# Two groups of attention heads share their transposes, and the largest scores run ten steps ahead instead of six

## The chip, the cores and the metric

The kernel runs on one core of a Trainium2 chip. A core has engines that each work through their own queue in order and wait for one another by semaphores: TensorE (PE in the profile, its weight loads PEld), VectorE (DVE), ScalarE (ACT), GpSimd (POOL), and SyncE (SP), which issues most of the DMA transfers. PE writes to PSUM, a small memory of eight banks; DVE and ACT read PSUM, POOL doesn't here. The metric is the device time of one execution in microseconds (us); the runs of a kernel are given by their median.

## The reference

Two transformer blocks with adaptive layer norm over x of 8 batches x 512 tokens x 128 channels, all in fp32. Only the first block's attention is touched:

```python
h = _layernorm(x) * (1 + ca) + sa
Q = lora(h, Wq...).reshape(N, S, 16, 8)          # 16 heads of 8 channels; K and V alike
energy = einsum("nqhd,nkhd->nhqk", Q, K) / sqrt(8)
attn = softmax(energy, axis=-1)
out = einsum("nhqk,nkhd->nqhd", attn, V).reshape(N, S, 128)
x = x + ga * lora(out, Wo...)
```

After it come a mixture of experts (8 experts, the best 2 for each token, and a shared one), a state-space layer and a second mixture of experts with a small feed-forward part. The softmax is computed as exp(score - largest score of the query) divided by the sum of these.

## The kernel before

**Groups, steps and slots.** A batch `b` has 16 heads. Four of them make a group: in group `g = 4b + m` the heads are 4j + m for j = 0 to 3, and head j uses the partitions 32j to 32j + 31 of PE, so the four heads of a group are four row groups of the array. There are 32 groups. A group has four steps, one for each 128 keys (`t = 4g + kc`), and a step has two slots (`s = 2t` and `2t + 1`), one for each half of the heads. `slot(s)` (L893) writes one slot: `scores` (two matmuls 32x512 of keys by queries, tile `ps`), `maxima` for a later step (two matmuls of queries by keys, tile `pm`, in the two row groups that the scores leave free), the two exponentials on ACT (`exps`, tile `es`), the reduction of `pm` on DVE to the largest score, and then everything that was put behind this slot.

**The order of the rest** is written out by hand: `at_slot(s, do)` (L606) appends a piece of work to slot s, and within a slot pieces stand in the order in which they were appended. All engines get their instructions in this order (`keep_in_program_order`), and each waits for its own operands only.

**Largest scores.** `LEAD = 6` (L286): in step t the maxima of step t + 6 are computed. Before step 0 the first six steps' maxima are done alone by `maxima_first` (L495), four matmuls and three reductions each. `split(g)` (L465) makes the group's queries `qt` and keys `kt` by masking `qf` and `kf`, 8 rows of each 32 in use; one spare row of `kt` (at `r0`) is set to 1. The reductions write into the columns of `mpad`, a tile that is zero elsewhere. `max_done(g)` (L514), in slot 8g - 3, transposes the group's `mpad` with four matmuls (`pmt`) and subtracts the result from `qt` on DVE, so that the spare row of `qt` holds minus the largest score, which the score matmul then adds. There are four `mpad` tiles and three buffers each for `qt` and `kt`.

**Weighted sums.** `values(b)` (L451) puts the values of a batch into `vaug`, 32 columns for each head: 8 values, a 1 in column 8 (it gives the sum of the exponentials), and zeros. `weigh(g, qc)` (L544) multiplies the exponentials by it, 16 matmuls for each 128 queries (tile `av`), and ACT copies the result (32 rows for each head, 9 of them in use) into `part`. This is done in slots 9, 11, 12 and 13 from the group's first. `normalise(g)` (L564), in slot 8g + 15, transposes `part` with four matmuls (`ppt`); DVE takes the reciprocal of the sums and multiplies.

**Around it**, for each batch: `load_stats`, `load_root`, `load_batch` (layer norm: DVE statistics, POOL square root and scaling `xh`, PE transposes `ptn`, ACT modulation `ht`), `project_batch` (`pqk`, then ACT makes `qf` and `kf`), `values` (`pv`), `channels_back` and `out_proj` (`pot`, `py`), `out_stats`, and then the routing for the experts: `tokens` (POOL and ACT), `turn` (`ptf`), `route` (`pl`), `choose`, `place` (`pcount`), and eight `scatter`s, indirect DMA transfers that POOL issues every second slot. `table` (L797) makes the list of expert blocks in slots 237 to 255.

**PSUM.** The pool `sc` has four buffers of a bank (`bank`), which `ps`, `av`, `pmt`, `ppt` and most other matmuls take in turn; `mx` has two buffers of two banks (`pair`) for `pm` and `pqk`.

Two lines set the number of steps ahead and where the two transposes stand:

```python
            at_slot(8 * g - 3, lambda g=g: max_done(g))          # L611
            at_slot(8 * g + 15, lambda g=g: normalise(g))        # L614
```

Of the kernel before, what the change touches and what calls it, by code (L numbers as in the profile page):

```python
# [10 lines left out]
FP = mybir.dt.float32  # L11
# [3 lines left out]
ALU = mybir.AluOpType  # L15
# [4 lines left out]
P = 128  # L20
# [48 lines left out]
def tile_adaln_two_blocks(  # L69
# [211 lines left out]

    mv1, rs1 = new_stats("l0a")
    mv2, rs2 = new_stats("l0f")
    LEAD = 6  # L286
    STEPS = 4 * 4 * B
    ES = 28
    kp = ctx.enter_context(tc.tile_pool(name="kp", bufs=1, side="right"))
# [2 lines left out]
    with tc.tile_pool(name="at", bufs=2) as at, tc.tile_pool(name="sc", bufs=4, space=PSUM) as psc, tc.tile_pool(  # L292
# [5 lines left out]
        for i in range(2):  # L298
            va = ate.tile([P, NC4, 16, 32], FP, tag=f"vaug{i}", name=f"vaug{i}")
            G.memset(va, 0.0)  # L300
            G.memset(va[:, :, :, HD], 1.0)
            vaugs.append(va)

        def pair(name):
# [5 lines left out]
        def flat(ps):  # L310
            return ps.rearrange("p c t -> p (c t)")
# [139 lines left out]
        def values(b):  # L451
            ht = batch[b]["ht"]
            ps = bank("pv")
            for c in range(NC4):
                pin(
                    T.matmul(
                        ps[:, c, :], lhsT=ht[:, c * P : (c + 1) * P], rhs=wqk[:, 2, :], start=True, stop=True
                    )
                )
            A.copy(  # L460
                vaugs[b % 2].rearrange("p c h r -> p (c h) r")[:, :, 0:HD],
                flat(ps).rearrange("p (c d) -> p c d", d=HD),
            )

        def split(g):  # L465

            b, m = g // 4, g % 4
            sp = (m + 1) % 4
            qt = ate.tile([P, S], FP, tag="qt", name="qt", bufs=3)
            kt = ate.tile([P, S], FP, tag="kt", name="kt", bufs=3)  # L470
            (V if g == 0 else G).tensor_scalar(qt, batch[b]["q"], mask[:, m : m + 1], zero, ALU.mult, ALU.add)
            G.tensor_scalar(kt, batch[b]["k"], mask[:, m : m + 1], spare[:, sp : sp + 1], ALU.mult, ALU.add)
            group[g] = (qt, kt)

        def maxima(u, half):

            g, qc = u // 4, u % 4
            qt, kt = group[g]
            r0 = HD * ((g + 1) % 4)
            pm = pair("pm")  # L480
            for i in range(2):
                r = 32 * (2 * half + i)
                pin(
                    T.matmul(  # L484
                        pm[:, i, :],
                        lhsT=qt[r : r + 32, qc * P : (qc + 1) * P],
                        rhs=kt[r : r + 32, :],
                        start=True,
                        stop=True,
                    )  # L490
                )
            mp = mpads[g % 4][:, qc, :].rearrange("p (j r) -> p j r", r=32)
            return lambda: V.tensor_reduce(mp[:, 2 * half : 2 * half + 2, r0], pm, AX.X, ALU.max)

        def maxima_first(u):  # L495

            g, qc = u // 4, u % 4
            qt, kt = group[g]
            r0 = HD * ((g + 1) % 4)
            pm = pair("pm")  # L500
            banks = [pm[:, 0, :], pm[:, 1, :], flat(bank("pm")), flat(bank("pm"))]
            for j, ps in enumerate(banks):
                r = 32 * j
                pin(
                    T.matmul(
                        ps, lhsT=qt[r : r + 32, qc * P : (qc + 1) * P], rhs=kt[r : r + 32, :], start=True, stop=True
                    )
                )
            mp = mpads[g % 4][:, qc, :].rearrange("p (j r) -> p j r", r=32)
            V.tensor_reduce(mp[:, 0:2, r0], pm, AX.X, ALU.max)  # L510
            for j in (2, 3):
                V.tensor_reduce(mp[:, j : j + 1, r0], banks[j], AX.X, ALU.max)

        def max_done(g):  # L514

            qt, _ = group[g]
            pt = bank("pmt")
            for c in range(NC4):
                pin(T.transpose(pt[:, c, :], mpads[g % 4][:, c, :], ident))  # L519
            V.scalar_tensor_tensor(qt, flat(pt), -1.0, qt, ALU.mult, ALU.add)  # L520

        def scores(t, half):
            g, kc = t // 4, t % 4
# [20 lines left out]
        def weigh(g, qc):  # L544

            b, m = g // 4, g % 4
            q = slice(P * qc, P * qc + P)
            ps = bank("av")
            for kc in range(NC4):
                for j in range(4):  # L550
                    pin(
                        T.matmul(  # L552
                            ps[32 * j : 32 * j + 32, 0, :],
                            lhsT=vaugs[b % 2][:, kc, 4 * j + m, :],
                            rhs=es_of[4 * g + kc, j][:, q],
                            start=(kc == 0),
                            stop=(kc == NC4 - 1),
                        )
                    )
            if qc == 0:  # L560
                part_of[g] = at.tile([P, NC4, P], FP, tag="part", name="part")
            A.copy(part_of[g][:, qc, :], ps[:, 0, :])

        def normalise(g):  # L564

            b, m = g // 4, g % 4
            part = part_of.pop(g)
            pt = bank("ppt")
            for c in range(NC4):
                pin(T.transpose(pt[:, c, :], part[:, c, :], ident))  # L570
            if m == 0:
                batch[b]["o"] = at.tile([P, NC4, D], FP, tag="o", name="o", bufs=1)
            p4 = pt.rearrange("p c (j r) -> p c j r", r=32)
            rd = stat.tile([P, NC4, 4], FP, tag="rd", name="rd")
            V.reciprocal(rd, p4[:, :, :, HD])
            o4 = batch[b]["o"].rearrange("p c (j m d) -> p c j m d", j=4, m=4)[:, :, :, m, :]
            V.tensor_tensor(o4, p4[:, :, :, 0:HD], rd.unsqueeze(3).to_broadcast([P, NC4, 4, HD]), ALU.mult)

        def channels_back(b):
            o = batch[b]["o"]  # L580
# [25 lines left out]
        def at_slot(s, do):  # L606
            after.setdefault(s, []).append(do)

        for g in range(4 * B):
            at_slot(8 * g - 16, lambda g=g: split(g))  # L610
            at_slot(8 * g - 3, lambda g=g: max_done(g))  # L611
            for qc in range(NC4):
                at_slot(8 * g + (9, 11, 12, 13)[qc], lambda g=g, qc=qc: weigh(g, qc))
            at_slot(8 * g + 15, lambda g=g: normalise(g))  # L614

        at_slot(-42, silu_c)
        for t, n in ((-41, 9), (-31, 5), (-22, 3), (-16, 8), *((t, 5) for t in range(-11, 0, 2))):
            at_slot(t, lambda n=n: keep_busy(n))
        at_slot(-34, low_rank)
        at_slot(-33, lambda: modulation(0, mod0))  # L620
        at_slot(1, lambda: clamp(mod0, MOE_SCALE))
        at_slot(2, out_bias)
        at_slot(-9, lambda: modulation(1, mod1))
        at_slot(6, lambda: clamp(mod1, None))
        rows = ((gab, gab_rows), (mod0[:, 2, :], ga_rows), (mod0[:, 3, :], sb_rows), (mod0[:, 4, :], cb_rows))
        for i, (src, dst) in enumerate(rows):
# [1 line left out]
            at_slot(8 + i, lambda dst=dst, i=i: mod_rows_in(dst, i))  # L628
        for b in range(B):
            for c in range(NC4):  # L630
                at_slot(32 * b - 40 + c, lambda b=b, c=c: load_stats(b, c))
            if b == 0:
                at_slot(-35, lambda: load_root(0, 0))
                at_slot(-32, lambda: load_root(0, 1))
            else:
                at_slot(32 * b - 35, lambda b=b: load_root(b))
            for i, s in enumerate((-30, 20, -24)):
                at_slot(32 * b + s, lambda b=b, i=i: load_batch(b, i))
            for i in range(2):
# [1147 lines left out]
```

## Time and profile before

| | |
|---|---|
| three runs, median (lowest to highest) | 1055.69 us (1055.5 to 1057.73) |
| the profiled execution | 1081.55 us |
| its span, mean clock granted to PE | 1079.6 us, 0.97 |
| busy in the span: PE, DVE, ACT, POOL | 1004.6, 668.8, 637.0, 486.7 us |
| first maxima at, first scores at | 18.51, 37.40 us |
| one batch of 32 slots in the steady part | 63.8 us |
| experts' first block begins | 548.7 us |

A row of a group reads: line, engine, operation, output <- inputs, shape and count, then busy time and mean ns of one, then idle time of the engine ahead of it and what ended it. L65 is the helper through which DVE, ACT, POOL and SP instructions are recorded, so these are told apart by their tiles. In windows, a row is start and end, length, busy time of PE, PEld, DVE, ACT and POOL with counts, then granted clock, DMA share and GB/s. In the chain of waits and the timeline, a row begins with start and duration in us. An fp32 matmul appears as two records, a transpose as one.

### The profile page before, as it was taken

Reading aid. Unit: us, or ns where it says so; the run is one execution under the profiler, and the core shown is the slowest. Engines: PE = TensorE matmul, PEld = TensorE weight load, DVE = VectorE, ACT = ScalarE, POOL = GpSimd, SP = SyncE. Lnnn points to the kernel's source line nnn. Section 1 sums busy time; section 2 is a strip of 40 time slices with the busy share of each in tenths; the row PEclk is TensorE's granted clock in tenths of the full one; section 3 lists DMA queues with packets and bytes.
Section 4 is the critical chain, followed back from the end, with each engine's and each line's share of the span. In section 5 each row is a group of like instructions: output and inputs, shape, how many; then the busy total and the mean of one; then the engine's idle time right before and its main releaser. Section 6 shows DMA issues by size and latency. Waiting matters only on the chain.

```text
span 1079.6 us, 24180 instructions
## 1 busy us (share of the span) xinstructions
PE 1004.6 (93%) x9522; PEld 658.2 (61%) x9522; DVE 668.8 (62%) x1297; ACT 637.0 (59%) x1400; POOL 486.7 (45%) x764
## 2 busy tenths in 40 slices
PE   9999999999999999999989999869899967767988
PEld 7555555555555555555579899748778634344556
DVE  6967787777768777777321123035766359888663
ACT  1466676666767666676745656225586563675554
POOL 3313142554627445454453133546441374666662
PEclk9999999999999999999999999969999968999999
DMA  6099200000000000000237796412553043213051
GB/s 168 20 315 283 88 12 2 11 22 2 31 1 20 13 9 24 2 30 10 71 114 221 230 275 196 127 35 64 146 152 89 8 131 99 79 59 126 23 186 39
DMA packets 94769, 95.36 MB, mean 88 GB/s; under 512 B 7664, under 2 KB 72560, under 8 KB 94656
## 3 DMA queue, kind: packets, MB, share of 16 engines
q1 hardware_dynamic: 90384, 85.13, 26.4%
q0 software_dynamic: 4096, 8.40, 2.6%
q8 instruction: 75, 1.23, 0.5%
q10 hardware_dynamic: 176, 0.30, 0.1%
q14 instruction: 38, 0.31, 0.1%
HBM read 62.43 MB, written 31.36 MB: 87 GB/s over the span
## 4 chain that ended last, share of the span: by engine, by line
PE 75%; DVE 10%; POOL 5%; ACT 4%; issue 4%; DMA 1%; SPq 0%; DVEq 0%; ACTq 0%; POOLq 0%
PE ps L531 21%; PE av L552 11%; PE pyb L1044 9%; PE ph L1033 8%; PE pm L484 3%; PE pmt L519 2%; PE r L1441 2%; PE pw L1352 2%; PE ppt L570 2%; DVE t L65 1%; DVE xc L65 1%; PE idle L417 1%; PE pe L1453 1%; PE pqk L444 1%; PE pyb L1003 1%
## 5 line engine op out<-in xcount | busy, mean ns | idle before, releaser
L65 DVE TENSOR_REDUCE mpad<-pm 128x2 f32<-128x1024 f32 (+1 forms) x262 | 310.3, 1194 | 110.2 <-PE pm L484 107.1
L65 ACT ACTIVATE es<-ps 128x512 f32<-128x512 f32 x512 | 275.6, 598 | 158.7 <-PE pm L484 135.0
L531 PE MATMUL ps<-qt,kt 32*128 32x512 f32 x1024 | 291.2, 630 | 0.7 <-DVE x L65 0.6
L484 PE MATMUL pm<-kt,qt 32*128 32x512 f32 x976 | 261.5, 636 | 0.0
L552 PEld LDWEIGHTS av<-es,vaug 128*32 128x32 f32 x4096 | 104.2, 109 | 94.1 <-ACT part L65 42.5
L552 PE MATMUL av<-es,vaug 128*32 128x128 f32 x4096 | 137.7, 276 | 0.0
L531 PEld LDWEIGHTS ps<-qt,kt 32*128 32x128 f32 x1024 | 94.0, 183 | 61.4 <-issue 30.6
L65 ACT ACTIVATE hid<-ph,bias 128x256 f32<-128x256 f32 x184 | 72.3, 478 | 58.0 <-PE ph L1033 56.2
L786 POOL DMA_INDIRECT x_rows<-tok,ux x64 | 65.0, 1015 | 68.4 <-DMA x_rows<-tok,ux 61.8
L1044 PEld LDWEIGHTS pyb<-w2b,hid 128*128 128x128 f32 x736 | 91.1, 194 | 5.8 <-ACT hid L65 2.4
L1044 PE MATMUL pyb<-w2b,hid 128*128 128x128 f32 x736 | 91.9, 278 | 2.6 <-ACT hid L65 2.0
L1033 PE MATMUL ph<-xt,w1b 128*128 128x256 f32 x368 | 89.9, 388 | 1.7 <-issue 1.7
L1064 POOL DMA_INDIRECT yg<-y_rows,yrows x64 | 63.3, 989 | 38.1 <-DMA hl<-h_chan 19.0
L484 PEld LDWEIGHTS pm<-kt,qt 32*128 32x128 f32 x976 | 73.1, 183 | 8.7 <-ACT kf L65 5.4
L1453 PE MATMUL pe<-x,l1w_sb 128*128 128x512 f32 x128 | 70.4, 663 | 5.3 <-ACT ye L65 5.3
L1033 PEld LDWEIGHTS ph<-xt,w1b 128*128 128x128 f32 x368 | 68.3, 195 | 9.8 <-issue 2.1
L65 DVE COPY xt<-pxt 128x256 f32<-128x256 f32 x46 | 19.2, 419 | 88.8 <-PE pxt L958 77.2
L65 POOL TENSOR_SCALAR qt<-qf,mask,zero 128x512 f32<-128x512 f32 x31 | 23.9, 772 | 109.4 <-PE pm L484 92.9
L65 ACT ACTIVATE ye<-pe,pc 128x512 f32<-128x512 f32 x64 | 43.2, 684 | 36.9 <-PE pe L1453 34.6
L65 POOL TENSOR_TENSOR t<-t 128x512 f32<-128x512 f32 x34 | 48.0, 1413 | 23.3 <-DVE t L65 21.8
L65 DVE TENSOR_TENSOR t<-ye,gb 128x512 f32<-128x512 f32 x64 | 55.0, 882 | 2.6 <-POOL t L65 2.3
L1441 PE MATMUL r<-l1w_sb,t 128*128 128x128 f32 x240 | 34.3, 290 | 15.2 <-POOL t L65 11.9
(298 smaller groups left out, 1559.4 us busy)
## 6 DMA issues: line engine op xcount, KB each, us to landing
x_rows<-zeros SPq DMA_DIRECT2D x16, 1024.0 KB
gb<-g_rows SPq DMA_DIRECT2D x32, 512.0 KB
w1b<-in_w1t SPq DMA_DIRECT2D x46, 256.0 KB
w2b<-in_w2t SPq DMA_DIRECT2D x46, 256.0 KB
xg<-x_rows SPq DMA_DIRECT2D x46, 128.0 KB
y_rows<-yb SPq DMA_DIRECT2D x46, 128.0 KB
x<-in_x SPq DMA_DIRECT2D x8, 256.0 KB
h_chan<-hf SPq DMA_DIRECT2D x8, 256.0 KB
```

Source lines behind the costliest of these rows:

```text
L65: return lambda *args, **kwargs: self.pin(call(*args, **kwargs))
L484: T.matmul(pm[:, i, :], lhsT=qt[r : r + 32, qc * P : (qc + 1) * P], rhs=kt[r : r + 32, :], start=True, stop=True,)
L519: pin(T.transpose(pt[:, c, :], mpads[g % 4][:, c, :], ident))
L531: T.matmul(ps, lhsT=kt[r : r + 32, kc * P : (kc + 1) * P], rhs=qt[r : r + 32, :], start=True, stop=True)
L552: T.matmul(ps[32 * j : 32 * j + 32, 0, :], lhsT=vaugs[b % 2][:, kc, 4 * j + m, :], rhs=es_of[4 * g + kc, j][:, q], start=(kc == 0), stop=( ...
L570: pin(T.transpose(pt[:, c, :], part[:, c, :], ident))
L786: nc.gpsimd.indirect_dma_start(out=x_rows[h], out_offset=IndirectOffsetOnAxis(ap=chosen["ux", b][:, k, c : c + 1], axis=0), in_=half[h]["t ...
L1033: pin(T.matmul(ph[:, f, :], lhsT=it["w1"][:, f * P : (f + 1) * P], rhs=it["x"], start=True, stop=True))
L1044: T.matmul(py[:, c, :], lhsT=it["hid"][:, f, c * P : (c + 1) * P], rhs=it["w2"][:, f, :], start=(f == 0 and "shared" not in it), stop=(f = ...
L1064: nc.gpsimd.indirect_dma_start(out=gathered[b][:, k, c, :], out_offset=None, in_=y_rows[h], in_offset=IndirectOffsetOnAxis(ap=half[h]["yro ...
L1441: T.matmul(ffn[b]["r"][:, c, :], lhsT=x[:, c * P : (c + 1) * P], rhs=w, start=(start and c == 0), stop=stop, skip_group_check=True,)
L1453: pin(T.matmul(pe, lhsT=l1w_sb[:, 2 + e, :], rhs=x1s[b], start=True, stop=True))
```

## The change

Groups are taken in pairs, 2n and 2n + 1.

- The spare row of a group is moved by 16, (m + 2) mod 4 in place of (m + 1) mod 4, and both groups of a pair write their largest scores into one `mpad` (two tiles in place of four). `max_done` is called for even groups only, in slot 8g - 3: four transposes, then two subtractions, one for each group's `qt`.
- In `vaug` the heads of odd m have their values in columns 16 to 23 and the 1 in column 24. ACT copies the weighted sums of an even group into `part` as before; those of the odd group are added to the same `part` by DVE. `normalise` is called for even groups only, in slot 8g + 23, and handles both.
- For that the maxima of two groups must be known before the first begins: `LEAD` is 10, ten steps of `maxima_first` stand ahead of step 0 (with five idle matmuls behind each), `qt` and `kt` have four buffers, and `split` and all that it needs are put eight slots earlier (`values` six, `modulation(1)` four).

```diff
-    for m in range(4):
+    for m in range(2):
         mp = ct([P, NC4, P], f"mpad{m}")
...
-    LEAD = 6
+    LEAD = 10
...
-            G.memset(va[:, :, :, HD], 1.0)
+            for e in range(2):
+                G.memset(va.rearrange("p c (n e) r -> p c n e r", e=2)[:, :, :, e, 16 * e + HD], 1.0)
...
-            A.copy(
-                vaugs[b % 2].rearrange("p c h r -> p (c h) r")[:, :, 0:HD],
-                flat(ps).rearrange("p (c d) -> p c d", d=HD),
-            )
+            for e in range(2):
+                A.copy(
+                    vaugs[b % 2].rearrange("p c (n e) r -> p (c n) e r", e=2)[:, :, e, 16 * e : 16 * e + HD],
+                    flat(ps).rearrange("p (n e d) -> p n e d", e=2, d=HD)[:, :, e, :],
+                )
...
-            sp = (m + 1) % 4
-            qt = ate.tile([P, S], FP, tag="qt", name="qt", bufs=3)
-            kt = ate.tile([P, S], FP, tag="kt", name="kt", bufs=3)
+            sp = (m + 2) % 4
+            qt = ate.tile([P, S], FP, tag="qt", name="qt", bufs=4)
+            kt = ate.tile([P, S], FP, tag="kt", name="kt", bufs=4)
...
-            mp = mpads[g % 4][:, qc, :].rearrange("p (j r) -> p j r", r=32)
+            mp = mpads[g // 2 % 2][:, qc, :].rearrange("p (j r) -> p j r", r=32)
...
-                pin(T.transpose(pt[:, c, :], mpads[g % 4][:, c, :], ident))
-            V.scalar_tensor_tensor(qt, flat(pt), -1.0, qt, ALU.mult, ALU.add)
+                pin(T.transpose(pt[:, c, :], mpads[g // 2 % 2][:, c, :], ident))
+            for k in range(2):
+                qt, _ = group[g + k]
+                V.scalar_tensor_tensor(qt, flat(pt), -1.0, qt, ALU.mult, ALU.add)
...
+            if g % 2:
+                part = part_of[g - 1][:, qc, :]
+                V.tensor_tensor(part, part, ps[:, 0, :], ALU.add)
+                return
...
-            rd = stat.tile([P, NC4, 4], FP, tag="rd", name="rd")
+            rd = stat.tile([P, NC4 * 4, 2], FP, tag="rd", name="rd")
...
-            at_slot(8 * g - 16, lambda g=g: split(g))
-            at_slot(8 * g - 3, lambda g=g: max_done(g))
+            at_slot(8 * g - 24, lambda g=g: split(g))
+            if g % 2 == 0:
+                at_slot(8 * g - 3, lambda g=g: max_done(g))
+                at_slot(8 * g + 23, lambda g=g: normalise(g))
...
-            at_slot(8 * g + 15, lambda g=g: normalise(g))
-        at_slot(-42, silu_c)
-        for t, n in ((-41, 9), (-31, 5), (-22, 3), (-16, 8), *((t, 5) for t in range(-11, 0, 2))):
+        at_slot(-50, silu_c)
+        for t, n in ((-49, 9), (-39, 5), (-30, 3), (-24, 8), *((t, 5) for t in range(-19, 0, 2))):
             at_slot(t, lambda n=n: keep_busy(n))
...
-        at_slot(-9, lambda: modulation(1, mod1))
+        at_slot(-13, lambda: modulation(1, mod1))
...
-                at_slot(32 * b - 40 + c, lambda b=b, c=c: load_stats(b, c))
+                at_slot(32 * b - 48 + c, lambda b=b, c=c: load_stats(b, c))
...
-                at_slot(32 * b - 35, lambda b=b: load_root(b))
-            for i, s in enumerate((-30, 20, -24)):
+                at_slot(32 * b - 43, lambda b=b: load_root(b))
+            for i, s in enumerate((-38, 20, -32)):
                 at_slot(32 * b + s, lambda b=b, i=i: load_batch(b, i))
             for i in range(2):
-                at_slot(32 * b - 18 + i, lambda b=b, i=i: project_batch(b, i))
-            at_slot(32 * b + 2, lambda b=b: values(b))
+                at_slot(32 * b - 26 + i, lambda b=b, i=i: project_batch(b, i))
+            at_slot(32 * b - 4, lambda b=b: values(b))
```

More of the change, by code (lines that the diff above doesn't have):

```diff
@@ L478, in maxima @@
             qt, kt = group[g]
-            r0 = HD * ((g + 1) % 4)
+            r0 = HD * ((g + 2) % 4)
             pm = pair("pm")
@@ L498, in maxima_first @@
             qt, kt = group[g]
-            r0 = HD * ((g + 1) % 4)
+            r0 = HD * ((g + 2) % 4)
             pm = pair("pm")
@@ L508, in maxima_first @@
                 )
-            mp = mpads[g % 4][:, qc, :].rearrange("p (j r) -> p j r", r=32)
+            mp = mpads[g // 2 % 2][:, qc, :].rearrange("p (j r) -> p j r", r=32)
             V.tensor_reduce(mp[:, 0:2, r0], pm, AX.X, ALU.max)
@@ L514, in max_done @@
         def max_done(g):
-            qt, _ = group[g]
             pt = bank("pmt")
             for c in range(NC4):
-                pin(T.transpose(pt[:, c, :], mpads[g % 4][:, c, :], ident))
-            V.scalar_tensor_tensor(qt, flat(pt), -1.0, qt, ALU.mult, ALU.add)
+                pin(T.transpose(pt[:, c, :], mpads[g // 2 % 2][:, c, :], ident))
+            for k in range(2):
+                qt, _ = group[g + k]
+                V.scalar_tensor_tensor(qt, flat(pt), -1.0, qt, ALU.mult, ALU.add)
         def scores(t, half):
@@ L572, in normalise @@
                 batch[b]["o"] = at.tile([P, NC4, D], FP, tag="o", name="o", bufs=1)
-            p4 = pt.rearrange("p c (j r) -> p c j r", r=32)
-            rd = stat.tile([P, NC4, 4], FP, tag="rd", name="rd")
+            p4 = pt.rearrange("p c (j e r) -> p (c j) e r", j=4, e=2)
+            rd = stat.tile([P, NC4 * 4, 2], FP, tag="rd", name="rd")
             V.reciprocal(rd, p4[:, :, :, HD])
-            o4 = batch[b]["o"].rearrange("p c (j m d) -> p c j m d", j=4, m=4)[:, :, :, m, :]
-            V.tensor_tensor(o4, p4[:, :, :, 0:HD], rd.unsqueeze(3).to_broadcast([P, NC4, 4, HD]), ALU.mult)
+            o4 = batch[b]["o"].rearrange("p c (j m d) -> p (c j) m d", j=4, m=4)[:, :, m : m + 2, :]
+            V.tensor_tensor(o4, p4[:, :, :, 0:HD], rd.unsqueeze(3).to_broadcast([P, NC4 * 4, 2, HD]), ALU.mult)
         def channels_back(b):
@@ L609, in tile_adaln_two_blocks @@
         for g in range(4 * B):
-            at_slot(8 * g - 16, lambda g=g: split(g))
-            at_slot(8 * g - 3, lambda g=g: max_done(g))
+            at_slot(8 * g - 24, lambda g=g: split(g))
+            if g % 2 == 0:
+                at_slot(8 * g - 3, lambda g=g: max_done(g))
+                at_slot(8 * g + 23, lambda g=g: normalise(g))
             for qc in range(NC4):
                 at_slot(8 * g + (9, 11, 12, 13)[qc], lambda g=g, qc=qc: weigh(g, qc))
-            at_slot(8 * g + 15, lambda g=g: normalise(g))
-        at_slot(-42, silu_c)
-        for t, n in ((-41, 9), (-31, 5), (-22, 3), (-16, 8), *((t, 5) for t in range(-11, 0, 2))):
+        at_slot(-50, silu_c)
+        for t, n in ((-49, 9), (-39, 5), (-30, 3), (-24, 8), *((t, 5) for t in range(-19, 0, 2))):
             at_slot(t, lambda n=n: keep_busy(n))
-        at_slot(-34, low_rank)
-        at_slot(-33, lambda: modulation(0, mod0))
+        at_slot(-42, low_rank)
+        at_slot(-41, lambda: modulation(0, mod0))
         at_slot(1, lambda: clamp(mod0, MOE_SCALE))
         at_slot(2, out_bias)
-        at_slot(-9, lambda: modulation(1, mod1))
+        at_slot(-13, lambda: modulation(1, mod1))
         at_slot(6, lambda: clamp(mod1, None))
@@ L630, in tile_adaln_two_blocks @@
             for c in range(NC4):
-                at_slot(32 * b - 40 + c, lambda b=b, c=c: load_stats(b, c))
+                at_slot(32 * b - 48 + c, lambda b=b, c=c: load_stats(b, c))
             if b == 0:
-                at_slot(-35, lambda: load_root(0, 0))
-                at_slot(-32, lambda: load_root(0, 1))
-            else:
-                at_slot(32 * b - 35, lambda b=b: load_root(b))
-            for i, s in enumerate((-30, 20, -24)):
+                at_slot(-43, lambda: load_root(0, 0))
+                at_slot(-40, lambda: load_root(0, 1))
+            else:
+                at_slot(32 * b - 43, lambda b=b: load_root(b))
+            for i, s in enumerate((-38, 20, -32)):
                 at_slot(32 * b + s, lambda b=b, i=i: load_batch(b, i))
             for i in range(2):
-                at_slot(32 * b - 18 + i, lambda b=b, i=i: project_batch(b, i))
-            at_slot(32 * b + 2, lambda b=b: values(b))
+                at_slot(32 * b - 26 + i, lambda b=b, i=i: project_batch(b, i))
+            at_slot(32 * b - 4, lambda b=b: values(b))
             at_slot(32 * b + 42, lambda b=b: channels_back(b))
```

## The prediction

> **What bounds the kernel now.** Read first: busy time by engine, then the windows of one stage each, because the change touches the attention alone.
>
> ```profile
> PE 1004.6 (93%) x9522; PEld 658.2 (61%) x9522; DVE 668.8 (62%) x1297; ACT 637.0 (59%) x1400; POOL 486.7 (45%) x764
> ...
> 18.50:37.40 18.90, 18.89 (x124) 12.18 (x124) 16.17 (x30) 0.37 (x1) 5.68 (x11) 1.00 0.00 1
> 261.00:325.00 64.00, 63.97 (x860) 34.55 (x848) 47.80 (x71) 43.55 (x95) 33.36 (x65) 1.00 0.04 14
> ```
>
> The second window is one batch: PE 63.97 of 64.00 us, DVE 47.80, ACT 43.55, clock 1.00. Taken at its word PE has no gap, and each microsecond removed from it is gained. The Trainium skill warns here (Perfetto Trace Analysis, Tensor Engine Instruction: the end of a matmul in the profile is modelled, not observed). So I read starts, in the chain of waits, in one stretch between the last weighted sum of a group (slot 5) and the first of the next (slot 9):
>
> ```profile
> 267.65 1.01 PE av L552 x32
> 268.66 0.59 PE pmt L519 x4
> ...
> 271.18 0.58 PE ppt L570 x4
> 271.76 1.27 PE ps L531 x3
> ...
> 274.56 1.01 PE av L552 x32
> ```
>
> A slot of scores and maxima takes 1.06 us after other work and 0.86 after another slot (starts in PE's timeline). Content of the stretch: 1.01 + 0.59 + 1.06 + 0.86 + 0.58 + 1.06 + 0.86 = 6.02 us. It lasts 6.91: 0.9 is waiting that busy time hides. Added over a batch (stretches from slot 1 to 5 and from 5 to 9: 8.41 + 7.20, 8.04 + 10.63, 7.29 + 6.92, 7.10 + 8.25 = 63.84 us) some 3 us are waits for DVE or ACT to free PSUM. So PE bounds the steady part, but not alone. By busy time the change would be worth its whole PE content; by starts only what those waits let through.
>
> The groups (busy, mean ns):
>
> ```profile
> L65 DVE TENSOR_REDUCE mpad<-pm 128x2 f32<-128x1024 f32 x250 | 303.2, 1219 | 110.2 <-PE pm L484 107.1 <-PE pm L505 2.7
> L65 ACT COPY part<-av 128x128 f32<-128x128 f32 x128 | 34.4, 269 | 10.6 <-PE av L552 9.6
> L65 DVE SCALAR_TENSOR_TENSOR qt<-pmt,qt 128x512 f32<-128x512 f32 x32 | 22.1, 690 | 12.0 <-PE pmt L519 11.1 <-POOL var L65 0.5 <-issue 0.3
> L570 PE MATMUL ppt<-ident,part 128*128 128x128 f32 x128 | 21.2, 287 | 1.3 <-ACT part L65 1.3
> L519 PE MATMUL pmt<-ident,mpad 128*128 128x128 f32 x128 | 21.0, 287 | 0.0
> L65 DVE TENSOR_TENSOR o<-ppt,rd 128x128 f32<-128x128 f32 x32 | 9.3, 291 | 1.1
> ```
>
> **Part 1, transposes removed.** 32 sets of four become 16 of each kind: 16 x 0.59 + 16 x 0.58 = 18.7 us of PE, 2.34 per batch. What of it is gained depends on the stretch.
>
> Even groups lose `pmt` at slot 5 and keep `ppt` at slot 7. DVE, from the av start: its reduce of slot 6 can begin at 2.27 instead of 2.86 us, with 1.14 per reduce behind it, then reciprocal and product (0.55; twice as wide, so some 0.15 more), and the second score of slot 9 needs the bank that these free. Before that bank is free at 5.7, after at 5.25: gain 0.46 of 0.59.
>
> Odd groups keep `pmt`, now with two subtractions on DVE (2 x 0.69), and lose `ppt` with its bank. DVE: subtractions to 3.1, reduces to 4.2 and 5.4 or 5.7. In the stretches with `ptf`, `pl` or `py` between the slots PE is later than that anyway, so `ppt` is gained whole.
>
> **Part 2, eviction of odd groups by DVE.** 64 copies leave ACT (64 x 0.269 = 17.2 us) and 64 additions of the same shape come to DVE, which read PSUM. The nearest row is `o<-ppt,rd`, 0.291: 18.6 us, 2.3 per batch, so DVE goes from 47.8 of 63.8 to some 50 of 61. A rule speaks against it: the Trainium skill (Perfetto Trace Analysis, Optimizing Scalar/DVE Operations) puts the fixed cost on PSUM at about 125 ns for DVE and 51 for ScalarE, so moving 64 evictions would add 64 x 0.074 = 4.7 us; the rows differ by 0.022, 1.4 us in all, and I take the rows. Either is off the path: the addition waits for its av, the next reduce stands behind it, but that reduce waits for maxima that end about 1 us after the av. The bank is needed 2.1 us after the av ends. Cost 0; without that cover 64 x 0.29 = 18.6 us.
>
> **Part 3, ten steps of lead.** In the steady part maxima cost PE nothing: the four row groups run together (scores alone, after the maxima have ended, still take 1.06 us a slot). So four steps moved to the front save no PE time later and are paid in full:
>
> ```profile
> 18.51 1.14 PE L505 MATMUL pm<-kt,qt 32*128 32x512 f32 x8 [0.46 <-POOL kt L65]
> 20.89 1.79 PE L505 MATMUL pm<-kt,qt 32*128 32x512 f32 x8
> ...
> 27.55 1.79 PE L505 MATMUL pm<-kt,qt 32*128 32x512 f32 x8
> ...
> 37.40 0.70 PE L531 MATMUL ps<-qt,kt 32*128 32x512 f32 x2
> ```
>
> An undisturbed step takes 2.38 us (18.51 to 20.89): DVE 1.22 + 2 x 0.68, and PE's 1.1 + 1.3 of idle matmuls beside it. Four steps 9.5, second subtraction 0.7, the values of batch 0 (1.1 of PE, partly beside DVE) 0.6: **+10.8 us**; ends 9.5 (all else hidden) and 13 (each step like the 3.3 of the last).
>
> **Part 4, steps moved eight slots.** Projection lands in slots 6 and 7 of a batch instead of 14 and 15, away from `py`: its wait (the stretch of 10.63 holds 1.4 of it) goes along and shrinks a little. Values go to slot 28, `ptn` to slot 0: same content. The statistics of the next batch fall into slots 16 to 19, on top of the four of the batch behind: DVE has 0.82 instead of 0.41 beside each reduce; counted through, PE waits some 0.5 per batch there. POOL gets square root (2.6 us) in slot 21 and this in slot 26, in front of the two token products:
>
> ```profile
> 225.17 3.14 POOL L65 TENSOR_SCALAR xh<-x,mv_l0a,rstd_l0a 128x128 f32<-128x128 f32 x4
> ```
>
> Token products end at 216.70 in POOL's timeline, their transpose starts at 220.43: 3.7 us of room. POOL's own waits for its scatters' landing (1.5 each) swallow the square root; counted through, the products end about when PE arrives, 0 to 1 us late. No DMA issue changes its place in SP's queue; POOL's scatters keep their slots, now behind these steps.
>
> Steady batch: -2.34 of content, -0.9 of waits that the freed banks remove, +0.5 (statistics), +0.15 (POOL): **-2.6 us**; ends -1.2 (only the two `ppt` sets of the odd groups, 2 x 0.58, are gained) and -3.3 (all content, the 0.9 of waits, no new one). Six whole batches: -15.6. The first 33 slots have the same four sets less and the statistics more, but not the waits of token work to lose: -2.34 + 0.5, -1.8. The last batch up to slot 237 loses its values (1.1, done 6 slots earlier) and one `pmt`: -1.7.
>
> **Part 5, the tail.** Here DVE sets the pace, and POOL waits for it:
>
> ```profile
> 506.49 0.60 PE pmt L519 x4
> ...
> 519.42 1.13 DVE mpad L65
> ...
> 521.07 0.25 POOL var L65
> ...
> 552.53 1.60 PE py L595 x8
> ```
>
> The chain runs through DVE from 507.1 to 521.0, then mostly POOL until `py`. With four steps more lead the reduces of slots 238 to 243 (6 x 1.14 = 6.8) have been done; one subtraction (0.7) and two additions come in: POOL could start 5.2 earlier. PE's part of it shortens by 3.4. I take **-4.5**.
>
> **Sum:** +10.8 - 1.8 - 15.6 - 1.7 - 4.5 = **-12.8 us**. The profiled execution, 1081.55 us (span 1079.6), would become about 1068.7. Attention runs at clock 1.00, so microseconds carry over to the runs' median of 1055.69, which is 2.4% shorter: **1042.9**. What follows the attention only shifts.
>
> **Rivals.**
> A. Forecast: 1043, own range 1037 to 1049. Chance 0.58.
> B. *PE waits anyway.* The stretches from slot 5 to 9 are set by DVE and ACT, gains stay at 1.2 per batch: +10.8 - 0.9 - 7.2 - 0.9 - 4.5 = -2.7, 1053. For it: 0.9 hidden in 6.91. Against it: in that stretch DVE itself waits 0.29, 0.46 and 0.27 for PE. 0.18.
> C. *All of it arrives*, 3.3 per batch and 5.2 in the tail, lead-in 9.5: about -20, 1036. 0.10.
> D. *Slower: POOL late in slot 30.* The 3.14 + 2.6 us in front of the token products do not fit into POOL's waits: 5.7 - 3.7 of room + 1.3 (statistics later on DVE) = 3.3 us for each of six batches, 19.8: 1063. It decides from 12.8/6 = 2.1 us per batch. Against: POOL waits 3.1 for scatters in the same stretch. 0.14, with all other ways of being slower.
>
> **Numbers.** The measurement tells 0.2%, 2.1 us, from no change. A, C and most of B are faster: 0.81; the top of B within 0.2%: 0.05; slower 0.14. Range 1036 to 1057: half of C lies below, most of D above.
>
> **What would show it.** First scores near 48 instead of 37.40; `pmt` and `ppt` 64 records each; batches near 61.2; `part` additions on DVE near 0.29; reduces ending near slot 235; no PE wait before `ptf`. A batch at 62.5 or longer, or a lead-in over 33 us, would make it wrong.

## The result, and the profile after

The changed kernel takes 1050.03 us (median of 20 runs, 1048.12 to 1056.66), the kernel before 1056.67 beside it (20 runs, 1054.86 to 1063.4): a ratio of 0.9939, 95% interval 0.9924 to 0.9954, that is -6.4 us (-8.0 to -4.9). The forecast was -12.8. Direction and lead-in were right; half of the gain is missing.

The profiled execution took 1048.35 us (span 1046.5), that of before 1081.55. These 33 us are not the change: most of them come behind the attention, which ends only 7.3 us earlier, and 2.4 of the 7.3 come before the first maxima, where the `plr` matmuls of before take 2.07 us and those of after 1.12. What can be compared is the attention, where the granted clock is 1.00 in both from the first maxima to slot 237, and there each stage from its own first start. Busy time of the page, then windows of the lead-in and of one batch of the changed kernel (columns as in the windows shown of before):

```profile
PE 989.5 (95%) x9434; PEld 648.6 (62%) x9434; DVE 673.9 (64%) x1333; ACT 620.5 (59%) x1344; POOL 485.9 (46%) x764
```

```profile
16.09:45.74 29.65, 29.35 (x205) 19.15 (x205) 25.79 (x42) 1.93 (x3) 9.68 (x16) 1.00 0.05 17
231.58:293.78 62.20, 62.20 (x832) 33.27 (x829) 48.27 (x73) 41.20 (x86) 33.60 (x64) 1.00 0.04 14
```

The lead-in went from 18.89 to 29.65, a batch from 63.83 to 62.20, and PE is again "busy" for all of it. The groups of the changed kernel, by form:

```profile
L65 DVE TENSOR_REDUCE mpad<-pm 128x2 f32<-128x1024 f32 x246 | 297.6, 1220 | 99.6 <-PE pm L488 93.2 <-PE pm L509 4.5
L65 DVE SCALAR_TENSOR_TENSOR qt<-pmt,qt 128x512 f32<-128x512 f32 x32 | 20.6, 686 | 8.8 <-PE pmt L523 8.8
L65 DVE TENSOR_TENSOR part<-part,av 128x128 f32<-128x128 f32 x64 | 17.9, 279 | 22.1 <-PE av L558 19.8 <-ACT es L65 2.2
L65 ACT COPY part<-av 128x128 f32<-128x128 f32 x64 | 17.4, 271 | 4.4 <-PE av L558 3.7
L580 PE MATMUL ppt<-ident,part 128*128 128x128 f32 x64 | 10.7, 288 | 0.2 <-ACT es L65 0.2
L523 PE MATMUL pmt<-ident,mpad 128*128 128x128 f32 x64 | 10.4, 286 | 0.0
L65 DVE TENSOR_TENSOR o<-ppt,rd 128x256 f32<-128x256 f32 x16 | 6.8, 425 | 0.5
```

64 transposes of each kind are left, the additions take 279 ns where the copies take 271, and the product of two groups takes 425 where that of one took 291. The content is as forecast, so what is missing should be waits.

A way to see waits on an engine that is always "busy": take the starts of the weighted sums in PE's timeline (they stand in slots 9, 11, 12, 13 of each group, that is in slots 1, 3, 4, 5, 9 and so on of a batch) and subtract. The stages, worked out so from both traces:

| stage | before | after | difference | forecast |
|---|---|---|---|---|
| first maxima to first scores | 18.89 | 29.65 | +10.8 | +10.8 |
| first scores to slot 33 | 61.34 | 61.81 | +0.5 | -1.8 |
| six batches, slot 33 to 225 | 382.63 | 372.23 | -10.4 | -15.6 |
| slot 225 to 237 | 24.04 | 22.06 | -2.0 | -1.7 |
| slot 237 to the last `py` | 47.12 | 43.38 | -3.7 | -4.5 |
| sum | | | **-4.9** | **-12.8** |

The lead-in, steps of the first maxima in PE's timeline of after, is the one of before with four steps more:

```profile
16.09 1.14 PE L509 MATMUL pm<-kt,qt 32*128 32x512 f32 x8 [0.45 <-POOL kt L65]
17.16 1.38 PE L419 MATMUL idle<-ident 128*128 128x128 f32 x10
18.48 1.79 PE L509 MATMUL pm<-kt,qt 32*128 32x512 f32 x8
```

16.09 to 18.48 is 2.39 us a step. And the tail, in the chain of waits:

```profile
503.55 1.29 DVE qt L65 x2
...
538.98 0.78 PE ppt L580 x4
539.78 0.37 DVE rd L65
540.17 0.42 DVE o L65
...
544.75 0.42 POOL wo L65
545.22 1.16 PE py L605 x8
```

DVE leaves the chain soon after the subtractions at 503.55; from there PE sets it up to the last `ppt` at 538.98, where before it was POOL and its scatters (chain of waits of before):

```profile
525.58 2.35 DMA x_rows<-tok,ux
...
534.61 0.96 POOL x_rows L786
```

From 530 to 550 us the clock is 0.91 here and 1.00 in before, so this stage compares less well than the others. The profiles of e4 and e8 below, whose last slots hold the same program, have 1.00 there and take 42.10 and 41.71 for it, 5.0 and 5.4 less than before. With that the stages add up to -6.2 to -6.6.

### The profile page after: what moved, and what is told of

The parts are those of the page before. It is cut to its first block, busy times and chain, and to the rows that moved or that the text cites. A ratio compares the mean times of both kernels' runs of the same rounds, so it can differ in the third digit from the quotient of the medians.

```text
span 1046.5 us, 24006 instructions
## 1 busy us (share of the span) xinstructions
PE 989.5 (95%) x9434; PEld 648.6 (62%) x9434; DVE 673.9 (64%) x1333; ACT 620.5 (59%) x1344; POOL 485.9 (46%) x764
## 4 chain that ended last, share of the span: by engine, by line
PE 79%; DVE 9%; ACT 4%; POOL 4%; issue 3%; DMA 1%; SPq 0%; DVEq 0%; ACTq 0%; POOLq 0%
PE ps L537 23%; PE av L558 12%; PE pyb L1055 9%; PE ph L1044 8%; PE pm L488 4%; PE idle L419 2%; PE pw L1363 2%; PE r L1452 2%; PE pqk L446 1%; PE pm L509 1%; DVE xc L65 1%; DVE t L65 1%; PE pe L1464 1%; PE pyb L1014 1%; DVE q L65 1%
## 5 line engine op out<-in xcount | busy, mean ns | idle before, releaser
L488 PE MATMUL pm<-kt,qt 32*128 32x512 f32 x944 | 252.1, 633 | 0.9 <-ACT kf L65 0.9
L537 PEld LDWEIGHTS ps<-qt,kt 32*128 32x128 f32 x1024 | 99.3, 183 | 71.8 <-issue 31.1
L1044 PE MATMUL ph<-xt,w1b 128*128 128x256 f32 x368 | 87.0, 379 | 0.0
L1464 PE MATMUL pe<-x,l1w_sb 128*128 128x512 f32 x128 | 73.6, 690 | 4.2 <-ACT ye L65 4.2
L65 POOL TENSOR_TENSOR t<-t 128x512 f32<-128x512 f32 x34 | 47.8, 1409 | 23.1 <-DVE t L65 15.6
```

What stands on the lines that cost most here:

```text
L65: return lambda *args, **kwargs: self.pin(call(*args, **kwargs))
L488: T.matmul(pm[:, i, :], lhsT=qt[r : r + 32, qc * P : (qc + 1) * P], rhs=kt[r : r + 32, :], start=True, stop=True,)
L537: T.matmul(ps, lhsT=kt[r : r + 32, kc * P : (kc + 1) * P], rhs=qt[r : r + 32, :], start=True, stop=True)
L1044: pin(T.matmul(ph[:, f, :], lhsT=it["w1"][:, f * P : (f + 1) * P], rhs=it["x"], start=True, stop=True))
L1464: pin(T.matmul(pe, lhsT=l1w_sb[:, 2 + e, :], rhs=x1s[b], start=True, stop=True))
```

## Experiments

The same starts give the stretches of one batch. Each number is the mean over five batches from slot 33, "batch" is slot 65 to 97. Of the stretches left out, 1 to 5 and 25 to 29 pass `pv` from one to the other (8.40 and 7.10 with six steps of lead, 7.10 and 8.19 with ten), and the others differ by less than 0.1, but for 9 to 13 in e9 (8.30 in place of 8.05). Two columns also differ by content: with ten steps `pqk` (1.9) stands in 5 to 9 in place of 13 to 17, and `ptn` (0.5) in 29 to 33 in place of 5 to 9.

| kernel | total, us | ratio to before (95%) | batch | 5 to 9 | 13 to 17 | 17 to 19 | 21 to 25 | 29 to 33 |
|---|---|---|---|---|---|---|---|---|
| before | 1056.67 | 1 | 63.83 | 7.18 | 10.57 | 3.12 | 6.92 | 8.25 |
| e3 lead and moves only | 1066.47 | 1.0083 (1.0056 to 1.0111) | 64.08 | 9.37 | 8.24 | 3.35 | 6.92 | 8.72 |
| e2 + shared `pmt` | 1059.48 | 1.0016 (1.0004 to 1.0028) | 62.92 | 8.78 | 8.24 | 3.35 | 6.33 | 8.63 |
| e5 + DVE copies | 1060.77 | 1.0041 (1.0026 to 1.0057) | 63.11 | 8.79 | 8.23 | 3.55 | 6.32 | 8.64 |
| after (shared `ppt`) | 1050.03 | 0.9939 (0.9924 to 0.9954) | 62.20 | 8.79 | 7.65 | 3.65 | 6.65 | 7.89 |
| e4 statistics early | 1050.18 | 0.9926 (0.9900 to 0.9952) | 61.81 | 8.78 | 7.65 | 3.25 | 6.65 | 7.89 |
| e8 `kf` beside `qf` | 1047.51 | 0.9912 (0.9885 to 0.9939) | 61.94 | 8.53 | 7.65 | 3.64 | 6.65 | 7.89 |
| e9 `normalise` later | 1051.81 | 0.9961 (0.9942 to 0.9980) | 62.86 | 9.37 | 7.65 | 3.65 | 6.37 | 7.89 |
| e13 `normalise` twice | 1056.25 | 0.9978 (0.9963 to 0.9994) | 62.24 | 8.78 | 7.65 | 3.64 | 6.65 | 7.89 |
| e1 shared `ppt` only, six steps | 1056.48 | 0.9992 (0.9977 to 1.0006) | 63.77 | 7.37 | 10.57 | 3.32 | 7.18 | 7.49 |
| e6 before, `kf` beside `qf` | 1051.67 | 0.9955 (0.9944 to 0.9966) | 63.06 | 7.19 | 9.95 | 2.95 | 6.91 | 8.25 |
| e7 = e1 + e6 | 1045.70 | 0.9894 (0.9864 to 0.9924) | 62.51 | 7.37 | 9.36 | 3.25 | 7.17 | 7.50 |

### e1, e2, e3: one part at a time

The theory was that the sharing brings its content and that something else takes it back: the statistics of two batches on top of each other on DVE, or the additions. The rivals were that the sharing is worth less than its content, or that it depends on what stands around it.

e1, from the kernel before:

```diff
+            if g % 2:                       # in weigh
+                part = part_of[g - 1][:, qc, :]
+                V.tensor_tensor(part, part, ps[:, 0, :], ALU.add)
+                return
-            at_slot(8 * g + 15, lambda g=g: normalise(g))
+            if g % 2 == 0:
+                at_slot(8 * g + 23, lambda g=g: normalise(g))
```

with `vaug` and `normalise` as in the changed kernel and `LEAD = 6`.

> The kernel before with only the second sharing: odd groups are added to part on DVE, one set of ppt for two groups; six steps of lead and one set of pmt for each group stay. By the prediction's account (2 x 0.58 of PE in a batch, gained whole; additions on DVE free) it is faster than before by about 9 us (8 batches x 1.16), batch near 62.7, no change in the lead-in. Rival, the additions on DVE are not free: they delay the reduces and eat it, 0 to -4 us, batch 63.3 or more.

e2, the changed kernel without that:

> The changed kernel without the second sharing: ten steps of lead, shared pmt, everything moved eight slots, but each group has its own part, copied by ACT, and its own ppt. If the two sharings simply add up, it stands against the changed kernel as before stands against the kernel with only the second sharing: about +9 us on the changed kernel, so +2 to +3 on before. If the additions on DVE are what took half of the gain, it is no slower than the changed kernel (-6 us on before or better), with batches of 62.2 or less.

e3, e2 without the other sharing too (both groups of a pair still write one `mpad`, but each transposes it for itself):

```diff
-            if g % 2 == 0:
-                at_slot(8 * g - 3, lambda g=g: max_done(g))
+            at_slot(8 * g - 3, lambda g=g: max_done(g))
-            for k in range(2):              # in max_done
+            for k in range(1):
```

> The changed kernel with neither sharing: ten steps of lead and everything moved eight slots, 32 sets each of pmt and ppt. Prediction's account: lead-in +10.1, six batches at +0.65 (statistics 0.5, POOL 0.15), tail -4: about +10 us on before, batch near 64.5. If the moved steps are what took the missing gain (statistics of two batches one on top of the other on DVE), the batch is 65 or longer and the total +13 us or more; if the sharing is simply worth less than its PE content, the batch is at 63.8 to 64.3.

Measured: lead and moves cost +8.8 us (forecast's account: about +10), and the batch grows by only 0.25, so the moved steps are not where the gain went. Sharing `pmt` on top is worth 1.16 a batch, two sets of 0.59, in the stretches where they stood. Sharing `ppt` on top of that is worth 0.72: it gains 0.59 and 0.74 where the two sets stood (13 to 17 and 29 to 33) and gives back 0.30 (17 to 19) and 0.32 (21 to 25). But the same sharing on the kernel before (e1) is worth nothing, and the table shows where: the stretch from 29 to 33 gains 0.76, but 5 to 9, 17 to 19 and 21 to 25 give back 0.65, and the stretch from 13 to 17 stays at 10.57 although its `ppt` is gone. Parts do not add up; what a set is worth depends on the wait beside it. In e1 the wait in 13 to 17 is in the open (PE's timeline, then ACT's):

```profile
191.14 0.59 PE L533 MATMUL ps<-qt,kt 32*128 32x512 f32 x2
...
191.59 1.02 PE L533 MATMUL ps<-qt,kt 32*128 32x512 f32 x4
193.48 1.16 PE L486 MATMUL pm<-kt,qt 32*128 32x512 f32 x8 [0.88 <-ACT kf L65]
```

```profile
190.35 0.69 ACT L65 ACTIVATE qf<-pqk,bqs 128x512 f32<-128x512 f32 x1 [1.74 <-PE pqk L445]
...
191.77 1.08 ACT L65 ACTIVATE es<-ps 128x512 f32<-128x512 f32 x2 [0.62 <-PE pm L486]
192.74 0.69 ACT L65 ACTIVATE kf<-pqk,pc 128x512 f32<-128x512 f32 x1
```

`pqk` holds one of the two pairs of banks of `pm` until ACT has made `qf` and, a slot later and behind two exponentials, `kf`. The maxima of slot 16 need that pair. From the start of `pqk` to these maxima it is 5.05 us in e1 (188.43 to 193.48) and 5.05 in the kernel before (189.49 to 194.54), where `ppt` simply lay inside the wait.

### e6, e7, e8: taking the wait for kf away

The edit is one line; in e6 and e7 it is slot 14 of a batch (18), in e8 slot 6 (26):

```diff
             for i in range(2):
-                at_slot(32 * b - 18 + i, lambda b=b, i=i: project_batch(b, i))
+                at_slot(32 * b - 18, lambda b=b, i=i: project_batch(b, i))
```

> The kernel before with the second step of project_batch (kf on ACT) put into the same slot as the first (14), so that ACT makes qf and kf one after the other and pqk gives its two banks back before the maxima of slot 16 ask for them. Theory 'wait for kf': stretch from slot 13 to 17 falls from 10.57 by 0.9 to 1.4 us, 7 batches: -6 to -10 us on before. Rival, ACT is then late with the exponentials of slot 15: stretch within 0.3, total within 2 us.

> The kernel with only the second sharing (six steps of lead, 1056.48), kf put into slot 14 as well. If the ppt that is missing in slot 15 was worth nothing only because PE waits for kf one slot later, it becomes worth its 0.58 here: stretch from slot 13 to 17 near 8.6, against 9.2 to 9.7 of before with the same move, and total -3 us against that kernel. If it is worth nothing for another reason (DVE), the two stretches are equal.

> The changed kernel with kf put into the same slot as qf (slot 6 of a batch). Theory 'wait for kf': stretch from slot 5 to 9 falls from 8.79 to about 7.7, total -6 to -8 us on the changed kernel, 0.987 of before. Rival, ACT late with the exponentials of slot 7: stretch above 8.5, total within 2 us.

e6 gains 4.8 us on the kernel before that ran beside it, 0.62 in the stretch from 13 to 17, less than the 0.9 to 1.4 expected, and 0.17 in the next. ACT's timeline of e6 shows `kf` directly behind `qf`:

```profile
189.95 0.69 ACT L65 ACTIVATE qf<-pqk,bqs 128x512 f32<-128x512 f32 x1 [1.74 <-PE pqk L444]
190.53 0.68 ACT L65 ACTIVATE kf<-pqk,pc 128x512 f32<-128x512 f32 x1
```

e7 settles that stretch of e1: with the wait gone, the missing `ppt` of slot 15 is worth 0.59 (9.95 to 9.36), its full 0.58, while the other stretches give and take as in e1. The stretch is longer than the 8.6 expected, but the total falls by 6 us against e6, where 3 were expected. At 1045.70 us it is faster than the changed kernel, with six steps of lead.

e8 missed: 8.79 to 8.53 in place of 7.7. In the changed kernel the wait for `kf` was the last to end in this stretch, but another ends 0.26 before it. Which one, e8 alone does not say.

### e9, e10: does the bank of ppt set the pace?

```diff
-                at_slot(8 * g + 23, lambda g=g: normalise(g))
+                at_slot(8 * g + 25, lambda g=g: normalise(g))
```

> The changed kernel with normalise two slots later (slots 9 and 25 of a batch in place of 7 and 23), so that the 1.01 us of a weighted sum follow the ppt on PE while DVE works through its reduces, the reciprocal and the product and gives the bank back. Theory 'the bank of ppt': the wait of 1.2 us in the stretch from slot 21 to 25 and part of that from 5 to 9 go; sum of 21 to 27 and 5 to 11 (9.59 + 12.67 = 22.26) falls by 1 us or more, 7 us in all on the changed kernel. Rival, ACT sets these stretches (exponentials and tokens in slot 22 to 24, kf in slot 7): the sum changes by less than 0.4, total within 2 us.

e9 fell on the wrong side: a batch of 62.86, 0.66 more. PE's timeline of e9:

```profile
247.00 1.02 PE L537 MATMUL ps<-qt,kt 32*128 32x512 f32 x4
248.90 1.16 PE L488 MATMUL pm<-kt,qt 32*128 32x512 f32 x8 [0.88 <-ACT kf L65]
249.86 1.02 PE L537 MATMUL ps<-qt,kt 32*128 32x512 f32 x4
250.82 0.66 PE L580 MATMUL ppt<-ident,part 128*128 128x128 f32 x4
```

The wait for `kf`, 0.88, is in the open again, and `ppt` stands behind it. In the changed kernel `ppt` lies inside it, as the chain of waits there shows:

```profile
240.84 1.92 PE pqk L446 x4
242.75 0.63 PE ps L537 x2
243.82 0.59 PE ppt L580 x4
244.41 1.20 PE ps L537 x4
245.61 1.24 PE pm L488 x6
```

From `pqk` to the maxima of slot 8 it is about 4.8 us with `ppt` between (240.84 to 245.61) and without (244.11 to 248.90): `kf` sets it, and this `ppt` was free. In slot 9 it is not free: it stands ahead of the weighted sum and adds its 0.58 to 5 to 9, and the `pot` of slot 10, which needs its product, now waits (9 to 13 grows by 0.25):

```profile
253.97 0.63 PE L593 MATMUL pot<-ident,o 128*128 128x128 f32 x4 [0.42 <-DVE o L65]
```

Only 21 to 25 gains, 0.28. e10 is e7 with the same edit:

> Six steps of lead, only the second sharing, kf in slot 14 (1045.70), with normalise in slots 9 and 25. Theory 'the bank of ppt': as in the other run, 0.5 to 1 us less a batch, total 1038 to 1042. Rival, ACT: within 2 us of 1045.7.

1046.36 us, 0.9904 (0.9889 to 0.9918): no different from e7. Its batch is 0.2 shorter, and in the profile its tail is 2.9 longer (slot 237 to `py` 45.79 to 48.65), at a clock of 0.89 from 515 to 530 us where e7 has 1.00.

### e5, e4, e13: what the additions and the wider normalise cost

e5, e2 with the copies of odd groups on DVE:

```diff
-            A.copy(part_of[g][:, qc, :], ps[:, 0, :])
+            (V.tensor_copy if g % 2 else A.copy)(part_of[g][:, qc, :], ps[:, 0, :])
```

> The kernel with only the first sharing (1059.48), with the weighted sums of odd groups copied into part by DVE in place of ACT; every group keeps its own part and its own ppt. Theory 'moving the eviction to DVE costs', about 0.6 us a batch, in the stretches from slot 17 to 19 and 21 to 25: batch 63.5 in place of 62.91, total +4 to +5 us. Rival, the place of ppt is what costs and the eviction is free: 62.9, total within 1 us.

+0.19 a batch, +1.3 us in the medians (2.6 by the ratios, each of them uncertain by more than 1). A third of what was expected, and all of it in one stretch, from 17 to 19. DVE's timeline of the changed kernel shows why there: it has no gap.

```profile
201.37 0.29 DVE L65 BATCH_NORM_STATS2 bnst<-x 128x6 f32<-128x128 f32 x1
201.69 0.18 DVE L65 BATCH_NORM_AGGREGATE mv_l0f<-bnst 128x2 f32<-128x6 f32 x1
201.79 0.26 DVE L65 BATCH_NORM_STATS2 bnst<-x 128x6 f32<-128x128 f32 x1
202.08 0.18 DVE L65 BATCH_NORM_AGGREGATE mv_l0a<-bnst 128x2 f32<-128x6 f32 x1
202.18 1.19 DVE L65 TENSOR_REDUCE mpad<-pm 128x2 f32<-128x1024 f32 x1
203.29 0.28 DVE L65 TENSOR_TENSOR part<-part,av 128x128 f32<-128x128 f32 x1
```

Statistics of the batch behind (`mv_l0f`) and of the next (`mv_l0a`) stand between two reduces, and the addition comes on top. e4 moves the second kind away:

```diff
-                at_slot(32 * b - 48 + c, lambda b=b, c=c: load_stats(b, c))
+                at_slot(32 * b - (61 if b > 1 else 48) + c, lambda b=b, c=c: load_stats(b, c))
```

> The changed kernel with load_stats of batches 2 to 7 in slots 3 to 6 of a batch, where DVE has gaps between its reduces, in place of 16 to 19, where out_stats of another batch stand too. Theory 'pile-up on DVE': stretch from slot 13 to 21 falls from 15.54 to near its PE content of 14.2, so about -1 us in each of six batches, -6 us on the changed kernel. Rival, PE waits there for something else (banks freed by ACT): within 1 us of the changed kernel.

The stretch from 17 to 19 falls by 0.40 to 3.25, and with it the batch: this pile-up is real, but it costs 0.40 and not the 1.3 that I had read from 13 to 21 (15.54 less a content of 14.2); the stretch from 13 to 17 does not move. Its total (0.9926) cannot be told from the changed kernel's.

e13 does the reciprocal and the product of `normalise` twice:

> The changed kernel with the reciprocal and the product of normalise done twice in a row (same result), 0.77 us more on DVE each time, which holds the bank of ppt that much longer. Theory 'the wider normalise is what took back 0.3 in the stretch from slot 21 to 25': this stretch grows by 0.5 to 0.8 from 6.65, the one from 5 to 9 by less than 0.3, because kf sets it: batch 62.8 to 63.2, total +4 to +6 us. Rival, ACT (exponentials and tokens) sets both: no stretch grows by more than 0.1, total within 1.5 us.

Both theories fall in part. The batch is 62.24 against 62.20, the stretch from 21 to 25 is 6.65 in both: the wider `normalise` is not what made that stretch 0.32 longer. DVE's and PE's timeline of e13 in that stretch:

```profile
213.72 0.34 DVE L65 RECIPROCAL rd<-ppt 128x32 f32<-128x32 f32 x1
214.10 0.42 DVE L65 TENSOR_TENSOR o<-ppt,rd 128x256 f32<-128x256 f32 x1
214.56 0.36 DVE L65 RECIPROCAL rd<-ppt 128x32 f32<-128x32 f32 x1
214.95 0.42 DVE L65 TENSOR_TENSOR o<-ppt,rd 128x256 f32<-128x256 f32 x1
```

```profile
214.38 1.08 PE L537 MATMUL ps<-qt,kt 32*128 32x512 f32 x2
214.77 0.70 PE L488 MATMUL pm<-kt,qt 32*128 32x512 f32 x2
214.81 1.07 PE L537 MATMUL ps<-qt,kt 32*128 32x512 f32 x2
```

The scores and maxima of slot 25 start before the bank of `ppt` is given back at 215.37, so they do not wait for it. In the rows of weight loads (PEld), those of the third and the fourth score behind `ppt` stand 0.38 apart in the changed kernel, and in e13 too (214.38 and 214.76), the last of them after a wait for an exponential on ACT. In e5 they are one row of two loads. The changed kernel, then e5:

```profile
214.06 0.18 PEld L537 LDWEIGHTS ps<-qt,kt 32*128 32x128 f32 x1 [0.24 <-issue]
214.44 0.18 PEld L537 LDWEIGHTS ps<-qt,kt 32*128 32x128 f32 x1 [0.20 <-ACT es L65]
```

```profile
216.73 0.21 PEld L535 LDWEIGHTS ps<-qt,kt 32*128 32x128 f32 x2 [0.24 <-issue]
```

So the 0.32 looks like a wait for ACT. Why it is there is not shown: it may be that with one `ppt` in 16 slots the four banks come round in another order, and the score gets a bank that an exponential leaves late. No run here tries that by itself; the 0.32 stays open. Against the changed kernel e13's median is 6 us longer (4 by the ratios), and of that its profile shows 0.3 in the six batches and 3.2 from slot 237 to `py`. There the last `ppt`'s second `rd` and `o` stand in the chain, 0.8; the clock is 0.89 from 515 to 530 us, where the changed kernel has 1.00, and how much of the rest is the clock's is not measured.

### e11, e12, e14: the first slots, and all together

e11 puts the row of `gab` last, so that PE does not wait for its product on DVE behind slot 2:

```diff
-        rows = ((gab, gab_rows), (mod0[:, 2, :], ga_rows), (mod0[:, 3, :], sb_rows), (mod0[:, 4, :], cb_rows))
+        rows = ((mod0[:, 3, :], sb_rows), (mod0[:, 4, :], cb_rows), (mod0[:, 2, :], ga_rows), (gab, gab_rows))
```

> The changed kernel with the row of gab as the last of four in slots 3 to 6 in place of the first, so that PE does not wait for gab behind slot 2 (1.49 us in its trace), where values(0) stood before and filled the time. Theory 'moved values opened a wait': start of scores to slot 9 falls from 19.31 by 1.0 to 1.5 us; and if this wait is what lets the granted clock fall to 0.66 between 53 and 68 us, as in two of the profiles with ten steps of lead, it stays 1.00. Total -1 to -2.5 us on the changed kernel. Rival: DVE is late with its reduces anyway, 19.0 or more, total within 1 us.

First scores to slot 9: 18.74 in place of 19.31, a gain of 0.57 where 1.0 to 1.5 was expected. Total 1051.53 us, 0.9954 (0.9938 to 0.9971): not to be told from the changed kernel. Moving `values(0)` forward did uncover a wait of 1.49 there, but behind it stands the next one.

e12 has all four edits (`load_stats` moved from batch 3 on):

> The changed kernel with all four: kf beside qf, normalise in slots 9 and 25, gab last, load_stats of batches 3 to 7 in slots 3 to 6. If the waits are independent, batches near 60.3 to 61 and a total of 1036 to 1041; if freeing one only uncovers the next, batches of 61.5 and 1045.

1042.03 us, 0.9865 (0.9834 to 0.9895), batches of 61.01 (slot 65 to 97). The four together take 1.19 off a batch, where the three that act in it give 0.39, 0.26 and -0.66 alone: with `kf` early the later `normalise` gains (5 to 9 is 8.18, against 8.53 in e8) instead of losing. e14 leaves the last pair's `normalise` where it was:

```diff
-                at_slot(8 * g + 25, lambda g=g: normalise(g))
+                at_slot(8 * g + (25 if g < 4 * B - 2 else 23), lambda g=g: normalise(g))
```

> The version with all four changes (1042.03), with the last pair's normalise back in slot 23 from its even group's first, since in the tail no weighted sum follows to cover it: slot 237 to py falls from 46.23 to about 43.4, total -2 to -3 us, 1039 to 1040. Rival, POOL and the routing set the tail: within 1 us.

Slot 237 to `py` falls from 46.23 to 42.23 in the profiles, but the one of e12 has a clock of 0.86 to 0.93 there and that of e14 1.00, so the edit's own share is not measured. The ratio is 0.9849 (0.9829 to 0.9869), 1042.38 us: 16 us faster than before and clearly faster than the changed kernel, but not to be told from e12.

## Where the prediction was right and where it was wrong

- **Lead-in, +10.8.** Right: 10.76, at 2.39 us a step. In the total, e3's +8.8 contains it.
- **Content of the transposes, -2.34 a batch.** Right. `pmt` brought 1.16 (e3 to e2), `ppt` 0.59 + 0.74 (e2 to after). The working of part 1, 0.46 of 0.59 for the even groups because the bank of `ppt` sets the pace, was wrong (0.59 came), and the sum had not used it.
- **"-0.9 of waits that the freed banks remove".** This is the step that failed, and the largest share of what is missing: 5.4 us over six batches. The 0.9 was the difference of a stretch's length (6.91) and its content (6.02), and I took it for a wait for banks that the removed transposes had held. Where `pmt` went, its stretches became shorter by 0.59 each and not by a hundredth more: in e2 the stretch from 21 to 25 takes 6.33 for a content of 5.43, so the 0.9 is still there. In 5 to 9 the last wait is now that for `kf`, and in 21 to 25 the stretch gave 0.32 back. Only the stretch from 29 to 33 shows more than its content, by 0.16, and that need not be a bank: a slot behind another slot takes 0.2 less than one behind other work (0.86 against 1.06), and there two slots came together.
- **Projection: "its wait goes along and shrinks a little".** It went along, and did not shrink: 13 to 17 fell by 2.33, 5 to 9 grew by 2.19, and `pqk` itself and the `ptn` that left account for 1.7 and 1.4 of these, which leaves, as an estimate, 0.6 of wait at the old place and 0.8 at the new. But I did not follow what it does there. It stands next to the one `ppt` that stays, and hides it. In the kernel before it stood over a `ppt` that goes: there, sharing alone is worth nothing (e1).
- **Additions: "cost 0".** Wrong in size: the cover holds in all stretches but one, where DVE has no gap. e5 gives 0.19 a batch for the move to DVE, the changed kernel 0.30 in that stretch. For 64 evictions the difference of the rows was 1.4 us and the estimate from the rule of the Trainium skill (Perfetto Trace Analysis, Optimizing Scalar/DVE Operations) 4.7. In the rows themselves it came to 279 against 271 ns, 0.5 us in all. That e5's medians show 1.3 is luck: what they show is the eviction's own time on a DVE without a gap, and they are too uncertain to tell 1.4 from 4.7. My mistake was to put both off the path.
- **Moved steps, +0.65 a batch.** Mis-sized: 0.25 (e3), and nearly all of it (0.23) from 17 to 19, where the statistics stand. POOL's part did not come: the token products end at 225.46, 0.9 before `ptf` starts at 226.36, so rival D had no place.

```profile
224.18 1.28 POOL L65 TENSOR_TENSOR tok<-tok,sb_rows 128x512 f32<-128x512 f32 x1
```

- **First 33 slots, -1.8.** Wrong by 2.3: the moves cost 1.9 there (61.34 to 63.23 in e3), where I had 0.5. The values that filled the wait for `gab` are gone, and e11 gets 0.57 of that back; the projection of batch 1 now stands in slot 6 among the rows of the modulation, which no run tries. Sharing brings 1.4 of its 2.34.
- **Slot 225 to 237 and the tail, -1.7 and -4.5.** -2.0 and -3.7, and for the tail -5.0 and -5.4 in the two profiles with the clock at 1.00. DVE no longer sets it, as forecast; PE and the last `ppt` do. The 5.2 of part 5 has a slip: 6.8 - 0.7 - 2 x 0.29 is 5.5.

The sum for a batch: +0.25 (moves) - 1.16 (`pmt`) - 1.33 (`ppt`) + 0.30 (17 to 19) + 0.32 (21 to 25) = -1.62; -1.63 was measured. Against the forecast's -2.6, the waits are 1.4 worse (0.62 given back and 0.16 gained in place of the 0.9), the moved steps 0.4 better. The result lies between the forecast and rival B; B's reason, that PE waits anyway, holds for the waits and not for the content.

## What to carry to other kernels

A stretch that is longer than its content shows that there is a wait, not what it is for: before counting it as gained, find the instruction that ends it, and check that the change touches that one. Work that lies inside another wait is free, and removing it gives nothing until that wait goes (e1: 0 us, with one line about `kf` in front 6 us); so look for the cheap line first. Lead that has to be paid at the start is a fixed price: 10.8 us here, which e7 did without.

## What was not expected of the hardware

PE's speed in the first microseconds differs between executions: the same eight `plr` records took 2.07 us in the profiles of before and e9 and 1.12 in those of after and e1, and the first maxima come between 16.1 and 18.5 us. e2 and e5, alike up to there, show 18.50 and 16.09. The granted clock does not show it: from 4 to 8 us it is 1.00 in before and in after. In the stage behind the first scores two profiles (e4, e8) show a granted clock of 0.66, where the changed kernel and five others with the same wait in front (e2, e3, e5, e9, e13) show 1.00. Windows of e8 and of the changed kernel:

```profile
53.00:68.00 15.00, 14.31 (x60) 4.84 (x60) 8.23 (x17) 7.10 (x16) 1.53 (x2) 0.66 0.27 77
```

```profile
53.00:68.00 15.00, 13.66 (x110) 5.37 (x111) 10.33 (x18) 9.31 (x21) 1.54 (x2) 1.00 0.50 154
```

It begins right after PE's wait of 1.5 us for `gab`, and the time to slot 9 is 3.0 us longer in e8 (22.30 against 19.31) and 4.2 in e4 (23.49). e11, e12 and e14, with `gab` last, show 1.00 too, but so do most with the wait: whether it is the cause stays open.
